# A Mamba scan on four engines: which of its products run on GpSimd, who makes the joins, and where z's SiLU stands

## The chip, the core and the metric

The kernel runs on one core of a Trainium2 chip. It is written instruction by instruction: each engine (TensorE, VectorE, ScalarE, GpSimd) and SyncE's DMA queue carries out its own instructions in the order in which the program issues them, and semaphores hold an instruction back until what it reads is there and what it overwrites is no longer needed. The metric is the time of one execution on the device in microseconds; for several runs the median is given. In the profile TensorE is PE (its weight loads PEld), VectorE is DVE, ScalarE is ACT, GpSimd is POOL and SyncE is SP.

## What is computed

A two-layer model on a 64 x 64 image of 256 channels, all in float32. Layer 0 is convolutions followed by an attention over 4096 positions. Layer 1 treats the positions as 4096 tokens: a Mamba block that runs forward and backward over them, with a small MLP behind it, and then a mixture of two experts. The change touches the Mamba block alone. Cut to what matters, the reference there is

```python
xz = einsum(x, in_proj_w); xc, z = split(xz)           # 512 channels each
xc = silu(causal_conv4(xc))
dt, Bm, Cm = split(xc @ x_proj_w); dt = softplus(dt @ dt_proj_w + b)
dA = exp(dt[..., None] * A); dBx = dt[..., None] * Bm * xc[..., None]
h = dA_t * h + dBx_t                                   # 512 channels x 16 states, step by step over the tokens
y = sum_over_states(h * C_t) + xc * D
out = (y * silu(z)) @ out_proj_w
```

once with the tokens in order and once reversed. The two results are added (m), and a layer norm, two matrix products and another layer norm follow.

## The kernel before

**Iterations and slots.** The tokens are cut into 8 chunks of 512, and the two directions take turns, so `mamba_phase` runs over 16 iterations: iteration i works on direction i % 2. The 512 channels by 16 states of an iteration are cut into 32 slots (`slots`, `SPS` = 32): four channel tiles e, in each of them four groups of states k, in each of them two halves j. A slot holds 128 rows (32 channels by 4 states) twice over, as [128, 2, 512]. The slot's number within its iteration is called `at` in the code. All 512 slots run in one loop, and the loop body writes out the order of the work on every engine by hand: the scheduler adds semaphores, and moves nothing.

**What a slot n does.**

- *Input product* (`inflow`, L1931, GpSimd): u = dtx * B into one of three buffers `dbx`. It is issued two slots ahead, in slot n - 2, and a buffer comes free when the scan of slot n - 1 relative to the issue has ended.
- *Decays* (`decay`, L1921, ScalarE): two exponentials of 512 elements into one of two PSUM buffers `da`, issued one slot ahead.
- *Scan* (`recur`, L1942, VectorE): the recurrence over both halves in one instruction of 1024 elements.
- *Join* (`bring`, L1967, VectorE): the scan takes both halves in one run, so the second half of the next slot needs its old state added to its first column, a 128x1 addition into `dbx`. It is issued right behind scan n for slot n + 1, and only from iteration 2 on, when there is an old state. The value to add (`brought`) is prepared by `carry` on GpSimd and ScalarE in slots 9 to 11, 30 and 31.
- *State copy* (`keep`, L1973, ScalarE): the last column of the scan, one slot later, ahead of the decays.
- *Product* with C: in most slots on VectorE (`readout`, L1953), behind the scan and the join. The slots in the set `POOLED` have it on GpSimd (`pooled`, L1958); there the scan writes straight to an SBUF buffer `h` (four of them), and the product is issued one slot later, behind that slot's input product. These are called pooled slots here, and the others plain.
- *Sums over states* (`sum_states`, L1982, TensorE), two slots at a time; if the first of the two is pooled, they are issued one slot later. The *gate product* (`close`, L1991, VectorE) multiplies the finished y of a channel tile by silu(z), in slots 1, 9, 17 and 25.

The loop body carries the order, for example:

```python
inflow(n + 2)
if n > 0:
    keep(n - 1)
if n > 0:
    decay(n + 1)
recur(n)
```

**What runs in between.** `prepare` computes the next iteration's xc, dt and z in small steps, one per slot (five of them early, in the last five slots of the iteration before): input projection, four convolution blocks on TensorE in slots 3 to 6 with a ScalarE pass after each, xc's SiLU in slot 8 (L1392 with a table load before and one behind it, L1331), the pieces of dt in slots 12 to 27 (among them L1438, L1441 and L1447 on ScalarE, the dt product L1499 on GpSimd in slots 21, 23, 25 and 27, and its stores to HBM, L1503). z's SiLU stands in slot 28 (L2055, again with two table loads). `output` is the output projection of the iteration before, in slots 1 to 3 (L1557 on TensorE).

`load_dt` (L1542, SyncE's queue) reads the rows of dt and dt*x back from HBM, each spread over 128 partitions, into one of three buffers for each; such a load waits until the last reader of its buffer is done. The second load for the next iteration takes the buffer that the decay and the input product of slot 30 read last.

`tail` is what follows the Mamba block on a finished chunk: two layer norms and the MLP, spread over about two iterations. It moves on by one step per slot, and each step names the engine it needs; `FULL` lists for every engine the slots in which no such step may be taken.

## Time and profile before

| | |
|---|---|
| median of 3 runs | 4116.03 us |
| the runs | 4113.85, 4116.03, 4123.45 us |
| the profiled execution | 4112.53 us |
| its span (first to last instruction) | 4110.7 us |
| mean granted TensorE clock | 0.933 |
| first scan to last scan of the Mamba stage | 1934.0 to 3812.6 us |

One execution is profiled. In a row of instruction groups stand the line, engine, operation, what is written and read with shapes, the count, then the busy microseconds and the mean nanoseconds of one instruction, and last the engine's idle time just before them and what ended it. A row of the stage table has the stretch, its length, then busy time and count for PE, PEld, DVE, ACT and POOL, the granted clock, and the DMA engines' busy share and GB/s. A row of waits has who waited for whom: microseconds in total, times, longest. A row of the timeline has start and length in microseconds, engine, line, operation, and in brackets the idle time before it with its releaser. An instruction's start may lie up to 0.1 us before the end of the one ahead of it on the same engine.

### The profile page before, as it was taken

To read this page: it belongs to the slowest core of one execution; us is meant where nothing else is said; L and a number is where in the kernel's file an instruction comes from. 1 tells how busy PE (TensorE), PEld (TensorE's weight loads), DVE (VectorE), ACT (ScalarE), POOL (GpSimd) and SP (SyncE) were. 2 spreads that over 40 slices of the span, in tenths; PEclk is the share of its full clock that TensorE was granted. 3 is DMA by queue.
4 is the path that set the end of the run, shared out by engine and by line. 5 is a ranking of instruction groups with operands and counts; after the bars stand their busy time and mean duration, and the time that the engine had idled before them with its cause. 6 is when DMAs were issued, how large, how long until landed. Compare 5 with 4: busy or idle time off the path is not lost. (4 is left out here: it accounts for less than half of the span.)

```text
span 4110.7 us, 44059 instructions
## 1 busy us (share of the span) xinstructions
PE 3590.8 (87%) x14968; PEld 1196.7 (29%) x14968; DVE 3501.4 (85%) x3335; ACT 2568.4 (62%) x3841; POOL 1807.0 (44%) x1137
## 2 busy tenths in 40 slices
PE   6769888999999999997888888888888888886898
PEld 2324332222222222222222222222222222222444
DVE  8998777989888889877899999999999999999322
ACT  1111226988888878875777767677777767774222
POOL 3020000000000000002888888888988888888100
PEclk9889998999999999998889999999999999987999
DMA  6232215222322223214333344444334444442121
GB/s 208 93 101 94 81 58 157 51 64 61 66 62 59 61 63 63 53 40 145 126 105 108 108 137 121 131 126 124 115 111 109 140 119 128 126 127 80 57 62 55
DMA packets 164329, 399.98 MB, mean 97 GB/s; under 512 B 36997, under 2 KB 46469, under 8 KB 163838
## 3 DMA queue, kind: packets, MB, share of 16 engines
q1 hardware_dynamic: 137166, 304.26, 24.5%
q0 software_dynamic: 24624, 84.43, 8.9%
q10 hardware_dynamic: 2304, 8.39, 0.6%
q8 instruction: 119, 1.95, 0.2%
q14 instruction: 116, 0.95, 0.1%
HBM read 268.17 MB, written 79.56 MB: 85 GB/s over the span
## 5 line engine op out<-in xcount | busy, mean ns | idle before, releaser
L1931 POOL TENSOR_TENSOR dbx<-dtxr,b 128x1024 f32<-128x1024 f32 x512 | 1202.0, 2360 | 232.8 <-DVE dbx L1967 92.1
L1044 ACT ACTIVATE e<-sc 128x1024 f32<-128x1024 f32 x1024 | 994.2, 1023 | 166.4 <-PE sc L1037 141.7
L1942 DVE TENSOR_TENSOR_SCAN da<-da,state,dbx 128x1024 f32<-128x1024 f32 x400 | 940.3, 2351 | 52.6 <-ACT da L1921 43.9
L954 DVE TENSOR_TENSOR s<-s,e 128x1024 f32<-128x1024 f32 x768 | 880.2, 1218 | 19.2 <-ACT e L1044 18.7
L1921 ACT ACTIVATE da<-dtr,aneg 128x512 f32<-128x512 f32 x1024 | 708.3, 692 | 50.4 <-DVE h L1942 18.7
L1037 PE MATMUL sc<-q,kS 32*128 32x512 f32 x4096 | 647.9, 645 | 16.2 <-ACT e L1044 11.4
L961 PE MATMUL av<-e,vT 128*32 128x512 f32 x4096 | 552.5, 608 | 0.2
L977 POOL DMA_DIRECT2D s<-s x94 | 81.5, 874 | 943.0 <-DVE s L954 872.8
L1953 DVE TENSOR_TENSOR h<-da,c 128x1024 f32<-128x1024 f32 x400 | 488.7, 1222 | 5.0 <-DVE dbx L1967 0.6
L462 PE MATMUL cv<-v,u 128*128 128x512 f32 x928 | 412.8, 605 | 29.4 <-DVE pad L283 14.2
L1982 PE MATMUL y<-h,sel 128*32 128x512 f32 x2048 | 312.5, 627 | 40.1 <-POOL h L1958 20.3
L1037 PEld LDWEIGHTS sc<-q,kS 32*128 32x128 f32 x4096 | 211.0, 184 | 455.1 <-issue 249.4
L1342 PE MATMUL mm<-u,win 128*128 128x512 f32 x464 | 253.1, 685 | 84.7 <-ACT xp L1370 77.7
L1973 ACT COPY state<-da 128x2 f32<-128x2 f32 x399 | 64.5, 162 | 359.0 <-DVE h L1953 358.0
L1958 POOL TENSOR_TENSOR h<-h,c 128x1024 f32<-128x1024 f32 x112 | 263.5, 2353 | 46.9 <-ACT state L1973 46.9
L1942 DVE TENSOR_TENSOR_SCAN h<-da,state,dbx 128x1024 f32<-128x1024 f32 x112 | 262.5, 2343 | 25.2 <-ACT da L1921 13.6
L462 PEld LDWEIGHTS cv<-v,u 128*128 128x128 f32 x928 | 178.7, 194 | 261.3 <-issue 227.8
L560 DVE SCALAR_TENSOR_TENSOR acc<-pad,wdw_s,acc 128x768 f32<-128x768 f32 (+1 forms) x192 | 236.0, 1234 | 19.9 <-ACT acc L553 14.2
L1388 PE MATMUL mm<-xp,taps 128*128 128x512 f32 x480 | 212.7, 595 | 0.0
L143 POOL TENSOR_TENSOR ln_few<-ln_few,minus_half 128x4 f32<-128x4 f32 x29 | 34.5, 1190 | 397.7 <-DMA ln_few<-ln_row 259.4
L954 DVE TENSOR_TENSOR s<-e 128x1024 f32<-128x1024 f32 x128 | 152.0, 1219 | 58.6 <-ACT e L1044 58.5
L961 PEld LDWEIGHTS av<-e,vT 128*32 128x32 f32 x4096 | 81.8, 108 | 395.2 <-issue 385.9
(380 smaller groups left out, 3902.6 us busy)
## 6 DMA issues: line engine op xcount, KB each, us to landing
dtr<-dtd SPq DMA_DIRECT2D x128, 512.0 KB
dtxr<-dtd SPq DMA_DIRECT2D x128, 512.0 KB
s<-s POOLq DMA_DIRECT2D x94, 512.0 KB, 5.8
b<-bcd SPq DMA_DIRECT2D x64, 256.0 KB
c<-bcd SPq DMA_DIRECT2D x64, 256.0 KB
dtd<-dt SPq DMA_DIRECT2D x64, 256.0 KB
dtd<-few SPq DMA_DIRECT2D x64, 256.0 KB
u<-uv SPq DMA_DIRECT2D x24, 640.0 KB
```

The lines of the kernel that those rows point to most:

```text
L462: nc.tensor.matmul(rows4(ps), u[:, dy, P * ci : P * ci + P], v[:, dy : dy + HR, ci, :], start=dy + ci == 0, stop=dy == k - 1 and ci == CT - 1,
L954: nc.vector.tensor_tensor(z, x, y, ALU.add)
L961: nc.tensor.matmul(g.av[32 * h : 32 * h + 32, :], vT[:, kb, P * t + 32 * h : P * t + 32 * h + 32], es[h // 2][:, h % 2, :], start=kb == 0, ...
L1037: nc.tensor.matmul(ps[h // 2][:, h % 2, :], kS[r, t, P * kb : P * kb + P], q_t[r, t, :], start=True, stop=True,)
L1044: nc.scalar.activation(e, ps[i], AF.Exp)
L1342: nc.tensor.matmul(ps, win[d][:, t, P * e : P * e + P], u[:, t, ::-1] if d else u[:, t, :], start=t == 0, stop=t == CT - 1,)
L1921: nc.scalar.activation(da[:, v, :], dts[i, e, j][0][:, v, :], AF.Exp, scale=aneg[i % 2][:, a : a + 1])
L1931: nc.gpsimd.tensor_tensor(u, dts[i, e, j][1], bcs[i, k][0][:, None, :].to_broadcast([P, 2, N]), ALU.mult)
L1942: nc.vector.tensor_tensor_scan(das[n].rearrange("p v n -> p (v n)"), da.rearrange("p v n -> p (v n)"), u.rearrange("p v n -> p (v n)"), st ...
L1953: nc.vector.tensor_tensor(hs[n], das[n], bcs[i, k][1][:, None, :].to_broadcast([P, 2, N]), ALU.mult)
L1958: nc.gpsimd.tensor_tensor(hs[n], hs[n], bcs[i, k][1][:, None, :].to_broadcast([P, 2, N]), ALU.mult)
L1982: nc.tensor.matmul(ys[i, e][32 * j : 32 * j + 32, :], cx.sel, hs[n + j // 2][:, j % 2, :], start=False, stop=k == SQ - 1,)
```

## The change

Four things are edited. `POOLED` goes from seven slots to eight: 8 and 28 leave it, 0, 6 and 30 join it. In a pooled slot n the join for slot n + 1 is no longer issued on VectorE behind the scan; it is issued on ScalarE as an Identity activation with the old state as its bias, between the state copy and the decays. z's SiLU moves from slot 28 to slot 24 (not in iteration 0, where it stays). The slot lists that keep the tail's steps off ScalarE and GpSimd are rewritten: for ScalarE 24 and 25 stand in the place of 28, for GpSimd 1 and 7 in the place of 9 and 29.

By these lists the tail's steps fall, from its second run on, into other slots. In even iterations its VectorE reduction (L1620) goes from slot 4 to slot 10, its GpSimd multiplies (L149) from slots 3 and 22 to 6 and 29, its two ScalarE passes on the norm (L1587) from 23 to 30. In odd iterations the VectorE subtraction (L129) goes from slot 24 to 29, and the last two MLP additions (L1613) from 16 and 23 to 25 and 28.

```diff
@@ recur @@
-            bring(n + 1)
+            if n % SPS not in POOLED:
+                bring(n + 1)
@@ bring @@
-            x = us[n][:, 1, 0:1]
-            nc.vector.tensor_scalar(x, x, brought[i, e // 2][:, e % 2, j // 2, k : k + 1], None, ALU.add)
+            x, old = us[n][:, 1, 0:1], brought[i, e // 2][:, e % 2, j // 2, k : k + 1]
+            if (n - 1) % SPS in POOLED:
+                nc.scalar.activation(x, x, AF.Identity, bias=old)
+            else:
+                nc.vector.tensor_scalar(x, x, old, None, ALU.add)
@@ mamba_phase @@
-        POOLED = {4, 8, 10, 12, 16, 20, 28}
+        POOLED = {0, 4, 6, 10, 12, 16, 20, 30}
...
-            "ACT": {6, 7, 8, 9, 16, 17, 18, 19, 22, 28, 29, 31},
-            "POOL": {5, 9, 11, 13, 17, 21, 23, 25, 27, 29, 30, 31},
+            "ACT": {6, 7, 8, 9, 16, 17, 18, 19, 22, 24, 25, 29, 31},
+            "POOL": {1, 5, 7, 11, 13, 17, 21, 23, 25, 27, 30, 31},
@@ the loop over the slots @@
                 if n > 0:
                     keep(n - 1)
+                if at in POOLED:
+                    bring(n + 1)
                 if n > 0:
                     decay(n + 1)
                 recur(n)
...
-                if at == 28 and i + 1 < 2 * NCH:
+                if at == (24 if i > 0 else 28) and i + 1 < 2 * NCH:
                     for z in gots[i + 1]["z"]:
                         nc.scalar.activation(z, z, AF.Silu)
                     exp_and_log()
```

## The prediction

> **What bounds the kernel now.** First the page: busy shares, then the costliest groups.

> ```profile
> PE 3590.8 (87%) x14968; PEld 1196.7 (29%) x14968; DVE 3501.4 (85%) x3335; ACT 2568.4 (62%) x3841; POOL 1807.0 (44%) x1137
> ...
> L1931 POOL TENSOR_TENSOR dbx<-dtxr,b 128x1024 f32<-128x1024 f32 x512 | 1202.0, 2360 | 232.8 <-DVE dbx L1967 92.1
> L1942 DVE TENSOR_TENSOR_SCAN da<-da,state,dbx 128x1024 f32<-128x1024 f32 x400 | 940.3, 2351 | 52.6 <-ACT da L1921 43.9
> L1953 DVE TENSOR_TENSOR h<-da,c 128x1024 f32<-128x1024 f32 x400 | 488.7, 1222 | 5.0 <-DVE dbx L1967 0.6
> L1958 POOL TENSOR_TENSOR h<-h,c 128x1024 f32<-128x1024 f32 x112 | 263.5, 2353 | 46.9 <-ACT state L1973 46.9
> ```

> The Mamba stage runs from 1931 to 3815 us: 512 slots, each with one scan on VectorE (2.35 us) and one product (1.22 us on VectorE, 2.35 on GpSimd). The table of stages, taken from 2400 to 3600 us, and the waits of VectorE there show what limits it.

> ```profile
> 2400.00:3600.00 1200.00, 1016.66 (x2974) 340.76 (x2973) 1146.66 (x1004) 861.36 (x1580) 1022.33 (x539) 0.93 0.42 122
> ```
> ```profile
> DVE da L1942 <- ACT da L1921: 21.2, 15, 1.7
> DVE h L1942 <- ACT da L1921: 10.7, 10, 1.2
> ```

> VectorE is 96% busy, GpSimd 85%, ScalarE 72%. What VectorE waits for is mostly ScalarE's decays. So VectorE is the bound, with holes. I therefore read the timeline scan by scan. The first view is VectorE in slots 28 to 30 of iteration 6, the second ScalarE there, the third two scans of iteration 1, which has no joins.

> ```profile
> 2976.47 2.34 DVE L1942 TENSOR_TENSOR_SCAN h<-da,state,dbx 128x1024 f32<-128x1024 f32 x1
> 2978.73 0.19 DVE L1967 TENSOR_SCALAR dbx<-dbx,brought 128x1 f32<-128x1 f32 x1
> ...
> 2979.49 2.35 DVE L1942 TENSOR_TENSOR_SCAN da<-da,state,dbx 128x1024 f32<-128x1024 f32 x1
> ...
> 2984.38 2.36 DVE L1942 TENSOR_TENSOR_SCAN da<-da,state,dbx 128x1024 f32<-128x1024 f32 x1 [1.20 <-ACT da L1921]
> ```
> ```profile
> 2976.79 1.42 ACT L1921 ACTIVATE da<-dtr,aneg 128x512 f32<-128x512 f32 x2
> 2978.22 1.28 ACT L2055 ACT_TABLE_LOAD   x1
> 2979.52 2.00 ACT L2055 ACTIVATE z<-z 128x1024 f32<-128x1024 f32 x2
> 2981.54 1.28 ACT L1331 ACT_TABLE_LOAD   x1
> ...
> 2982.93 1.41 ACT L1921 ACTIVATE da<-dtr,aneg 128x512 f32<-128x512 f32 x2
> ```
> ```profile
> 2088.08 2.35 DVE L1942 TENSOR_TENSOR_SCAN h<-da,state,dbx 128x1024 f32<-128x1024 f32 x1 [1.99 <-PE y L1982]
> 2090.35 2.33 DVE L1942 TENSOR_TENSOR_SCAN da<-da,state,dbx 128x1024 f32<-128x1024 f32 x1
> ```

> From one scan's start to the next I read, over iterations 2 to 14 and without idle time: 3.52 to 3.60 us in a plain slot, 2.55 in a pooled one. In iteration 1 the same are 3.52 to 3.60 and 2.26. So a join costs nothing in a plain slot (the product behind it is ready to follow) and 0.29 in a pooled one, where the next scan stands behind it. An iteration takes 117.6 us, 4.4 of it idle: 1.41 in slot 29 (behind z's SiLU), 1.05 in slot 9 (behind xc's SiLU), 0.64 in slot 4, 0.57 in slot 19 (TensorE's sums), 0.41 in slot 0.

> **The change part by part**, per iteration, for iterations 2 to 15. The sum is made on the profiled execution: 4112.5 us, span 4110.7; the median shown is 3.5 above it.

> *One product more on GpSimd.* Pooled slots go from 7 to 8; each saves 3.58 - 2.55 = 1.03 on VectorE: **-1.0**. GpSimd gains 2.35 beside it. It is 85% busy, so 2.35 in some 115 us makes 88%; that cover fails only where GpSimd is already late, which is slot 0, below.

> *Eight joins on ScalarE.* 8 x 0.29 = **-2.3** on VectorE, if the next scan is not held up. ScalarE in a pooled slot: the state copy starts 0.12 after the scan, the two decays end 1.73 after it. A join goes between them. The trace has no such form; the nearest rows are the 128x1 copy at L1447 (0.16) and the 128x16 exponential at L1521 (0.20) on one side, the 128x512 Identity with bias at L1384 (0.69) on the other. I take 0.20, the nearest in size: decays end at 1.95, the next scan can start at 2.26. At 0.69 they end at 2.42 and each pooled slot loses 0.16, 18 us in all. Behind the join in ScalarE's queue stand decay n+1 and all that follows, and the join waits for GpSimd's input product n+1. That one ends, relative to the scan's start, at -3.3 in slot 4, -2.2 in 6, -3.0 in 10, -0.2 in 12 (at worst 0.9), -0.5 in 16, -2.2 in 20, -2.4 in 30 (medians), so it has been done by then. In slot 0 it ends at +2.0.

> [...]

> *z's SiLU from slot 28 to slot 24.* It is four instructions, 4.66 us on ScalarE (two table loads of 1.28, two SiLUs), and no DMA. Its old hole goes: **-1.4**. In slot 24 it stands ahead of a dt copy with its one-column copy (0.58 + 0.16), state copy 24, and decay 26 (1.42). With decay 25 ending 1.73 after scan 24, decay 26 ends at 1.73 + 4.66 + 0.74 + 0.17 + 1.42 = 8.75, where VectorE, with scan 24, 25 and the gate product of slot 25 (0.68), gets to scan 26 after 3.59 + 4.10 = 7.7, or 8.4 with a tail step in odd iterations. So a new hole of 0.35 to 1.05; and decays that run late, as in even iterations now (up to 3.6 after scan 24), make it 2.65. I take **+1.1**, as the tail step that causes the worst is moved away. GpSimd's dt product of slot 25 and the dtd stores of SP then wait some 3 us for that dt copy; the row-broadcast loads they precede are needed from slot 30 on, so this costs nothing; if it did, it would show in slot 0.

> *Slots 1 to 9.* Here plain VectorE time is not the bound: TensorE goes without a gap from the gate product of slot 1 through output projection and four convolution blocks of 3.5 us (8 matmuls each), then xc's SiLU (4.5 us on ScalarE), then decay 10. From the end of that product to scan 10 is 30.3 to 32.2 us in every iteration. The change saves VectorE 0.29 in slot 4, 1.3 in slot 6 and gives back 1.0 in slot 8; a 1.2 us reduction of the tail leaves slot 4 every second iteration and comes back in slot 10. That is 1.2 of savings a turn, of which the chain lets through only the wait of ScalarE's slot-8 state copy, 0.28 to 1.21, mean 0.6. The rest turns into idle time: **+0.6** (0 to 1.2).

> *The turn of the iteration.* Slot 0's second input row waits for a buffer that decay 30 frees, then for its DMA. The views are SP's issues and GpSimd in iteration 6.

> ```profile
> 2984.37 0.51 SPq L1542 DMA_DIRECT2D dtr<-dtd  x1
> 2984.97 0.56 SPq L1542 DMA_DIRECT2D dtxr<-dtd  x1
> ```
> ```profile
> 2990.84 7.00 POOL L1931 TENSOR_TENSOR dbx<-dtxr,b 128x1024 f32<-128x1024 f32 x3 [2.32 <-DMA dtxr<-dtd]
> ```

> From issue to use are 5.0 to 7.7 us (here 5.9). With the SiLU gone decay 30 ends 1.73 after scan 29 and no longer 4.85, but slots 29 and 30 also shrink, by 1.5 and 1.3. Input product 1 then ends 1.73 + 0.6 + 6.4 + 2.36 = 11.1 after scan 29, scan 32 is at 3.6 + 2.3 + 3.6 = 9.5 (10.7 with a tail step of 1.2): 0.4 to 1.6 into slot 0. Join, two decays and hand-overs add 1.75, now in series, where VectorE waited for the product alone before. Slot 0 takes 2.3 to 3.4 and at worst 4.7, mean 3.05, so idle 0.8 for 0.41: **+0.4** (-0.4 to +2). Then product 30 on GpSimd pushes input product 2 to 4.7 after input product 1; VectorE's join in slot 1 waits up to 0.75: **+0.5**. The sums of slot 30 now stand in slot 1 of TensorE's queue, ahead of that gate product; they are ready about 1 us before VectorE is.

> *Tail slots.* The tail's instructions are the same, moved by some slots; the 2.35 us GpSimd multiply falls into slots 6 and 29 for 3 and 22. Input products there are 1 to 3 us early, so nothing; without that lead 2.35 a turn at most.

> Sum: -1.0 - 2.3 - 1.4 + 1.1 + 0.6 + 0.4 + 0.5 = -2.1 an iteration, 14 iterations: -29.4. Iterations 0 and 1 have no joins and stalls of their own; I take 0. From 4116.0 that is **4086.6**. All good ends together give -4.75 an iteration (4050), all bad ones +1.9 (4143).

> [...]

> **The rivals.** *The joins block ScalarE (slower).* If the wait for GpSimd is later than I read, for instance on a later instruction of its queue, the decay and the next scan slip one for one. It speaks for it that GpSimd ends 0.8 to 1.2 after the scan in slots 11 and 13, between the pooled ones; against it the medians above. My slack is 0.3; beyond it, 0.3 of lateness in each of seven slots eats the 2.1. With 0.9 beyond the slack the iteration is 6.3 - 2.1 = 4.2 longer: 4175; with 0.45, 4130. Chance 0.13.

> *The turn takes it.* Late DMA and GpSimd's backlog, with slot 0 at 4.7 and slot 1 at its full 0.75 each time: +1.9 more, 4113. For it: the row's wait is in the trace already; against: decay 30 comes earlier. Chance 0.12.

> *TensorE hides it.* If the TensorE and ScalarE chain of slots 1 to 9 is fed from further back than slot 1, the gain before it is absorbed and only slots 10 to 24 keep theirs (4 x 0.29): -1.2 + 1.1, about 4115. Against: VectorE has no idle time in slots 21 to 28. Chance 0.11.

> *All good ends*, 4050 to 4060: chance 0.05. My forecast, 4062 to 4108: 0.59.

> **How the numbers follow.** A time within 0.2% (8.2 us) can hardly be told from no change. Faster: 0.59 + 0.05 + half of the second and some of the third, 0.72; same 0.12; slower 0.16. The range goes from 4060 to 4120.

> **What would show it.** Pooled slots of 2.26 with a ScalarE Identity 128x1 ahead of the decays; no hole in slot 29; a hole at scan 26 behind the SiLU; slots 1 to 9 nearly as long as before; idle time of VectorE near 5.6 an iteration. Long gaps ahead of the joins on ScalarE would make me wrong.

## The result: 26 us slower, where 29 us less was forecast

The changed kernel takes 4142.2 us (median of 5 runs, 4141.0 to 4153.7), the kernel before 4116.0. The ratio is 1.0076, with a 95% interval of 1.0059 to 1.0093. All runs below are given by such a ratio to the kernel before, and a difference in us between two of them is the difference of their ratios times 4116. The forecast was 4086.6 and its range ended at 4120. The profiled executions have spans of 4139.1 and 4110.7 us, 28.4 apart. Single executions of one kernel lie up to some 20 us apart (4104.8 to 4127.1 in one run below), so places are read from the one profiled execution, and gains from the ratios.

The page of the kernel after, first its busy shares, then the groups that answer to those shown of before (columns: line, engine, operation, tiles, shape, count, busy us, mean ns of one, then the idle time ahead of them and what ended most of it):

```profile
PE 3597.1 (87%) x14968; PEld 1194.4 (29%) x14968; DVE 3466.7 (84%) x3207; ACT 2571.2 (62%) x3953; POOL 1845.6 (45%) x1153
...
L1931 POOL TENSOR_TENSOR dbx<-dtxr,b 128x1024 f32<-128x1024 f32 x512 | 1203.4, 2362 | 172.7 <-DMA dtxr<-dtd 65.6
...
L1942 DVE TENSOR_TENSOR_SCAN da<-da,state,dbx 128x1024 f32<-128x1024 f32 x384 | 901.1, 2347 | 86.4 <-ACT da L1921 81.1
...
L1954 DVE TENSOR_TENSOR h<-da,c 128x1024 f32<-128x1024 f32 x384 | 469.0, 1221 | 4.6 <-DVE da L1942 0.5
L1986 PE MATMUL y<-h,sel 128*32 128x512 f32 x2048 | 316.2, 653 | 128.8 <-POOL h L1959 110.5
```

The same group of sums in the kernel before:

```profile
L1982 PE MATMUL y<-h,sel 128*32 128x512 f32 x2048 | 312.5, 627 | 40.1 <-POOL h L1958 20.3
```

VectorE has 34.7 us less to do (3501.4 before) and the scans of the plain slots wait more: 86.4 us where it was 52.6. New is the last line. TensorE's sums over states waited 20 us for GpSimd's products before, and 110 after.

From 2400 to 3600 us, the row of the stage table (PE, PEld, DVE, ACT and POOL busy, then clock, DMA share and GB/s) and the waits (total us, times, longest):

```profile
2400.00:3600.00 1200.00, 1005.81 (x2937) 335.51 (x2936) 1110.89 (x901) 858.17 (x1653) 1033.57 (x544) 0.92 0.40 121
```
```profile
PE y L1986 <- POOL h L1959: 76.7, 25, 7.9
ACT xc L1384 <- PE mm L1388: 66.4, 38, 3.2
DVE da L1942 <- ACT da L1921: 52.4, 30, 4.2
```

VectorE's idle time in this stretch is 89 us (1200 - 1110.9), before it was 53. The three waits can be read as one chain, which the runs below take apart: the sums wait for GpSimd, ScalarE's passes over the convolution (L1384) wait for TensorE (66.4; 27.6 before), and VectorE's scans wait for the decays behind those passes (52.4; 21.2 before).

The table sets the forecast's terms beside the trace. It gives the mean of iterations 3 to 14, per iteration, from scan start to scan start; idle time is VectorE's, and hand-overs of about 0.1 us beside a join (0.29 less the join's own 0.19) count as work.

| step of the prediction | forecast | measured |
|---|---|---|
| VectorE's own work (one product, eight joins) | -3.3 | -2.9 |
| hole in slot 29 goes | -1.4 | -1.4 |
| new hole behind z's SiLU (slots 23 to 25) | +1.1 | +0.5 |
| slots 1 to 9, idle | +1.1 | +2.5 (slot 6 alone +2.0) |
| slot 0, idle | +0.4 | +1.2 |
| slots 10 to 22, idle | 0 | +0.5 (slot 20 +0.8, slot 19 -0.5) |
| slot 31, idle | 0 | +0.7 |
| sum, from the unrounded terms | -2.1 | +1.0 |

That is 11.8 us over twelve iterations. Iteration 2 is 5.4 longer, iteration 15 4.9, iterations 0 and 1 together 2.9, and 3.5 lie outside; together 28.4. VectorE's idle time is 8.4 us an iteration, where the prediction had some 5.6.

VectorE behind z's SiLU, and from slot 28 on, in the iteration that the prediction shows (counted from 0 it is iteration 8; the prediction called it 6):

```profile
2984.26 2.36 DVE L1942 TENSOR_TENSOR_SCAN da<-da,state,dbx 128x1024 f32<-128x1024 f32 x1 [0.78 <-ACT da L1921]
...
2994.92 2.35 DVE L1942 TENSOR_TENSOR_SCAN da<-da,state,dbx 128x1024 f32<-128x1024 f32 x1
...
2998.51 2.34 DVE L1942 TENSOR_TENSOR_SCAN h<-da,state,dbx 128x1024 f32<-128x1024 f32 x1
3000.77 2.33 DVE L1942 TENSOR_TENSOR_SCAN da<-da,state,dbx 128x1024 f32<-128x1024 f32 x1
```

The hole is at scan 26 (0.78), scan 29 starts without one, and pooled slot 30 takes 2.26. So far the change does what was forecast. ScalarE's join behind scan 30:

```profile
2998.63 0.16 ACT L1977 COPY state<-da 128x2 f32<-128x2 f32 x1 [0.89 <-DVE h L1954]
2998.69 0.30 ACT L1969 ACTIVATE dbx<-dbx,brought 128x1 f32<-128x1 f32 x1
2998.88 1.41 ACT L1921 ACTIVATE da<-dtr,aneg 128x512 f32<-128x512 f32 x2
```

It takes 0.30 where the prediction took 0.20 from a row. The decays still end before the scan does (at 3000.29, the scan at 3000.85), as the sum had it.

### The profile page after: what moved, and what is told of

It is laid out like the page before. It is cut to its first block, busy times and chain, and to the rows that moved or that the text cites. A ratio compares the mean times of both kernels' runs of the same rounds, so it can differ in the third digit from the quotient of the medians.

```text
span 4139.1 us, 44001 instructions
## 1 busy us (share of the span) xinstructions
PE 3597.1 (87%) x14968; PEld 1194.4 (29%) x14968; DVE 3466.7 (84%) x3207; ACT 2571.2 (62%) x3953; POOL 1845.6 (45%) x1153
## 3 DMA queue, kind: packets, MB, share of 16 engines
q8 instruction: 119, 1.95, 0.2%
## 4 chain that ended last, share of the span: by engine, by line
PE 37%; DVE 14%; ACT 10%; issue 9%; DMA 3%; POOL 3%; SPq 0%; DVEq 0%; POOLq 0%; ACTq 0%
PE sc L1037 8%; DVE da L1942 8%; PE av L961 7%; PE mm L1388 5%; ACT da L1921 4%; PE mm L1557 3%; PE mm L2250 3%; PE o L2192 2%; DVE h L1954 2%; DVE h L1942 2%; PE y L1986 2%; DVE s L954 1%; PE mm L1435 1%; DMA dtxr<-dtd 1%; POOL dbx L1931 1%
## 5 line engine op out<-in xcount | busy, mean ns | idle before, releaser
L1931 POOL TENSOR_TENSOR dbx<-dtxr,b 128x1024 f32<-128x1024 f32 x512 | 1203.4, 2362 | 172.7 <-DMA dtxr<-dtd 65.6
L1942 DVE TENSOR_TENSOR_SCAN da<-da,state,dbx 128x1024 f32<-128x1024 f32 x384 | 901.1, 2347 | 86.4 <-ACT da L1921 81.1
L1921 ACT ACTIVATE da<-dtr,aneg 128x512 f32<-128x512 f32 x1024 | 706.9, 690 | 43.0 <-DVE h L1942 15.7
L1954 DVE TENSOR_TENSOR h<-da,c 128x1024 f32<-128x1024 f32 x384 | 469.0, 1221 | 4.6 <-DVE da L1942 0.5
L1942 DVE TENSOR_TENSOR_SCAN h<-da,state,dbx 128x1024 f32<-128x1024 f32 x128 | 299.8, 2342 | 33.1 <-ACT da L1921 21.6
L1959 POOL TENSOR_TENSOR h<-h,c 128x1024 f32<-128x1024 f32 x128 | 301.5, 2355 | 8.4 <-ACT state L1977 8.4
L1342 PE MATMUL mm<-u,win 128*128 128x512 f32 x464 | 237.3, 647 | 28.4 <-ACT xp L1370 20.8
```

Source lines behind the costliest of these rows:

```text
L1921: nc.scalar.activation(da[:, v, :], dts[i, e, j][0][:, v, :], AF.Exp, scale=aneg[i % 2][:, a : a + 1])
L1931: nc.gpsimd.tensor_tensor(u, dts[i, e, j][1], bcs[i, k][0][:, None, :].to_broadcast([P, 2, N]), ALU.mult)
L1942: nc.vector.tensor_tensor_scan(das[n].rearrange("p v n -> p (v n)"), da.rearrange("p v n -> p (v n)"), u.rearrange("p v n -> p (v n)"), st ...
L1954: nc.vector.tensor_tensor(hs[n], das[n], bcs[i, k][1][:, None, :].to_broadcast([P, 2, N]), ALU.mult)
L1959: nc.gpsimd.tensor_tensor(hs[n], hs[n], bcs[i, k][1][:, None, :].to_broadcast([P, 2, N]), ALU.mult)
```

## The turn: what stands in front of TensorE

The turn into iteration 8: TensorE in the changed kernel, GpSimd just before it, then TensorE in the kernel before:

```profile
2892.99 1.56 PE L1986 MATMUL y<-h,sel 128*32 128x512 f32 x8 [4.44 <-POOL h L1959]
2894.49 8.28 PE L1557 MATMUL mm<-xc,wout 128*128 128x512 f32 x16
...
2904.56 3.70 PE L1388 MATMUL mm<-xp,taps 128*128 128x512 f32 x8
```
```profile
2888.29 2.35 POOL L1931 TENSOR_TENSOR dbx<-dtxr,b 128x1024 f32<-128x1024 f32 x1 [2.41 <-DVE da L1942]
2890.60 2.34 POOL L1959 TENSOR_TENSOR h<-h,c 128x1024 f32<-128x1024 f32 x1
```
```profile
2875.30 2.84 PE L1557 MATMUL mm<-xc,wout 128*128 128x512 f32 x6
2881.24 1.12 PE L1557 MATMUL mm<-xc,wout 128*128 128x512 f32 x2 [3.10 <-DVE xc L1991]
...
2887.69 3.60 PE L1388 MATMUL mm<-xp,taps 128*128 128x512 f32 x8
```

Before, six passes of the output projection ran ahead of the gate product. After, the sums of slot 30 stand in front of all of it, and they wait for GpSimd's product 30, which stands in GpSimd's queue behind an input product that waits itself: 2.41 us here, for a buffer that a scan frees; 3.62 at the next turn, for its DMA. Only then does the projection start. The granted clock shows in the rows too: eight sums take 1.06 us elsewhere, 1.56 here and 1.9 at most turns. In iterations 3 to 14 a period of half clock (0.5 in the trace's record of the granted clock) begins in slots 0 to 2 in 11 of 12 iterations (61 us in all), before in 3 (10 us). The convolution starts 8.6 us after the end of the gate product; before, 7.2 in even and 6.5 in odd iterations (means of iterations 2 to 14).

Four runs alter this place. The first takes slot 28 instead of 30:

```diff
-        POOLED = {0, 4, 6, 10, 12, 16, 20, 30}
+        POOLED = {0, 4, 6, 10, 12, 16, 20, 28}
```

> The changed kernel with the pooled slots 0, 4, 6, 10, 12, 16, 20 and 28: 28 for 30, the number stays eight. Theory A: the sums of slot 30 are back in slot 0, TensorE is not held up, 1.6 to 2 us an iteration less: 4114 to 4120. Theory B: slot 0's join stays in series with the late input product; a plain slot 30 gives the DMA 1.3 us more, of which half shows: 4133. Theory C: no difference, 4142.

Measured: 1.0006 (0.9991 to 1.0022). One slot's number is worth 0.7%, some 29 us. In the profiled execution even iterations fall to 113.2 us (after 116.5, before 118.1), and there the convolution starts 6.4 after the gate product. Odd ones stay at 121.1 (after 120.9, before 117.3) and the convolution at 8.5: their slot 0 is still late, and the last sections return to it. The swap also takes a product from GpSimd at the turn. VectorE's wait for an input product in slot 1, 0.5 us an iteration in the changed kernel as forecast, goes with it, so the 29 us are not TensorE's order alone.

To see whether slot 0's serial join is the loss, slot 28 takes the place of slot 0, and then of both 0 and 30 (seven products):

```diff
-        POOLED = {0, 4, 6, 10, 12, 16, 20, 30}
+        POOLED = {4, 6, 10, 12, 16, 20, 28, 30}     # the one
+        POOLED = {4, 6, 10, 12, 16, 20, 28}         # the other
```

> The changed kernel with the pooled slots 4, 6, 10, 12, 16, 20, 28 and 30: 28 for 0. Theory A: the sums of slot 30 are still in slot 1 behind GpSimd, so the loss of slots 1 to 9 stays: 4135 to 4142. Theory B: slot 0's join is back on VectorE, decay 1 runs beside the input product; idle time of slot 0 goes from 1.6 to 0.4, 14 x 1.2 = 17 us less: 4125. Theory C: no difference.

> The changed kernel with seven pooled slots, 4, 6, 10, 12, 16, 20 and 28: neither 0 nor 30. One product an iteration goes back to VectorE (+1.0). Theories A and B together: both holes at the turn go, 1.6 + 1.2 - 1.0 = 1.8 us an iteration less, 4117 or below; the six joins on ScalarE that stay are worth 0.3 each against before, so it may fall below 4116. Theory C: 4142 or more.

Measured: 1.0071 (1.0051 to 1.0091) and 1.0033 (1.0019 to 1.0047). Without slot 0 in the set nothing is won while slot 30 is in it. Slot 0 itself loses 1.0 us of idle time (1.65 to 0.68), but slot 31 gains 0.7 and slot 4 0.8, the latter through a decay buffer (below), so this run alone doesn't clear slot 0. Without slot 30, slot 0's product on GpSimd is a gain: 1.0006 with it, 1.0033 without, with intervals that just overlap. So slot 30 in the set is a loss, and slot 0 without it is none.

Two runs keep slot 30 and mend TensorE's order. One puts three matmuls of the output projection ahead of the sums of slot 30, as they ran before:

```diff
                 for f in range(ET):
+                    if co == 0 and f == ET - 1:
+                        yield
...
+                if at == 1 and i > 0:
+                    out = output(i - 1)
+                    step(out)
                 if j == 2 and n > 2 and (n - 3) % SPS in POOLED:
                     sum_states(n - 3)
```

> The changed kernel with one thing moved: the first three of the four matmul pairs of the output projection's first half are issued ahead of the sums of slot 30 in TensorE's queue, not behind them. Nothing else differs. Theory A (the sums of slot 30, now in slot 1 and waiting for GpSimd's product 30, hold TensorE's queue up and start output projection and convolutions some 2 us later, so that scan 10 is late): the stretch from slot 1's gate product to scan 10 goes from 32.1 back to about 30.5 us, 14 x 1.6 = 22 us less, 4120. Theory B (the join of slot 0 on ScalarE, in series behind GpSimd's late input product, is the loss): no difference, 4142. Theory C (the SiLU in slot 24 and the moved tail steps): no difference, 4142.

Measured: 1.0051 (1.0039 to 1.0064), about 10 us back. Theory A had 22. The convolution still starts 8.2 to 8.3 after the gate product, and the half clock still begins there in 10 of 12 iterations. The other adds five matmuls ahead of the sums, whose result the true ones overwrite:

```diff
+                if co == 0:
+                    for v, f in enumerate((0, 1, 2, 0, 1)):
+                        nc.tensor.matmul(
+                            ps, wout[d][:, f, P * co : P * co + P], g[:, f, :], start=v == 0, stop=v == 4
+                        )
+                    yield
```

> The changed kernel in which TensorE is kept busy through the wait of slot 1: five extra matmul pairs of the output projection (into the same PSUM tile, overwritten by the true ones, so the result is the same) ahead of the sums of slot 30, and the first two true pairs between those sums and the gate product. Theory A2 (the wait for product 30 leaves TensorE idle, its granted clock halves for 3.4 to 10 us at the turn of every iteration, and the output projection and the first convolution run at half rate): no half clock in slots 0 to 2 any more; gate product to first convolution from 8.5 to about 6.5 us, and 14 x 1.6 to 2 us less than the changed kernel, which is 31 us above before: 4 to 9 us above before. Theory A1 (only the order in the queue counts, the clock does not): as the run that moved three pairs forward, 20 us above before, or more for the extra 4.7 us of matmuls.

Measured: 1.0033 (1.0015 to 1.0051), 18 us back and 14 above before, between the two theories. The half clock in slots 0 to 2 falls from 61 to 7 us and the convolution starts at 7.2 to 7.6. Between this run and the one above the intervals overlap, so how much of it is the clock and how much the order is not settled.

## Parts of the change alone

Only the joins on ScalarE, with the seven products, z's SiLU and the lists of before:

```diff
-            bring(n + 1)
+            if n % SPS not in POOLED:
+                bring(n + 1)
...
+            if (n - 1) % SPS in POOLED:
+                nc.scalar.activation(x, x, AF.Identity, bias=old)
...
+                if at in POOLED:
+                    bring(n + 1)
```

> The kernel before with the joins behind its seven pooled slots on ScalarE and nothing else of the change. My price of 0.29 a join where nothing else holds the next scan, in slots 10, 12, 16 and 20 (slots 4, 8 and 28 are followed by waits on TensorE's chain or on a SiLU): 4 x 0.29 x 14 = 16 us below before. Rival (the joins block ScalarE's queue): no gain, or above before.

Only the new tail lists:

```diff
-            "ACT": {6, 7, 8, 9, 16, 17, 18, 19, 22, 28, 29, 31},
-            "POOL": {5, 9, 11, 13, 17, 21, 23, 25, 27, 29, 30, 31},
+            "ACT": {6, 7, 8, 9, 16, 17, 18, 19, 22, 24, 25, 29, 31},
+            "POOL": {1, 5, 7, 11, 13, 17, 21, 23, 25, 27, 30, 31},
```

> The kernel before with the two new slot lists of the tail steps and nothing else of the change. Theory D (the moved tail steps put a DMA round trip and a GpSimd multiply into SP's and GpSimd's queues just before the turn, so the loads for slots 31 and 0 leave some 3 us late, and an MLP pass into pooled slot 20): idle time in slot 20 (odd) 1.5, in slot 31 (even) 1, in slot 0 (odd) 1 more: +1.8 us an iteration on average, 20 to 25 us above before. Rival (the steps are the same and lie where there is room): within 4 us of before.

And the kernel with 28 for 30, but with the old lists (the same lines the other way round):

> The changed kernel with 28 for 30 in the pooled set, and with the two slot lists of before. Against the same with the new lists (4 us above before or level with it): theory D: the odd iterations lose the idle time of slots 20, 29 and 0, the even ones that of slot 31, together 2 us an iteration, but the two norm passes are back in slot 23 right ahead of the SiLU, which costs 0.8: 14 x 1.2 = 17 us less, 13 to 17 us below before. Rival (the lists make no difference): level with before.

Measured: joins alone 1.0026 (1.0016 to 1.0036), lists alone 0.9991 (0.9979 to 1.0002), old lists with the SiLU in slot 24 1.0044 (1.0031 to 1.0058). The lists cost nothing by themselves, and the SiLU in slot 24 needs them: with the old ones tail steps stand beside it, slot 25 of even iterations takes 6.8 us and slot 0 7.5. So theory D was wrong in both runs.

The joins alone are a loss, where 16 us less had been expected, though pooled slots shrink as forecast (slots 8 and 10 from 2.55 to 2.27). Slot 20 of odd iterations gives the hint. It takes 3.88 us in this kernel and in the changed one, and 2.55 before. ScalarE in slot 20 of iteration 7 of the changed kernel:

```profile
2843.69 0.16 ACT L1977 COPY state<-da 128x2 f32<-128x2 f32 x1 [0.18 <-DVE h L1954]
2843.75 0.30 ACT L1969 ACTIVATE dbx<-dbx,brought 128x1 f32<-128x1 f32 x1
2845.95 1.42 ACT L1921 ACTIVATE da<-dtr,aneg 128x512 f32<-128x512 f32 x2 [1.90 <-DVE h L1942]
```

The decays of slot 21 wait 1.90 us for the end of scan 20, which they have no business with: there are two decay buffers, and slot 21 should use the one that slot 19 left. In the built program it doesn't. There the tile for slot 21 has the PSUM address of the tile of slot 20.

## The decay buffers do not take turns

The text on the kernel before says that the scheduler adds semaphores and moves nothing. It does one thing more, which I had not looked at: it picks one of the two `da` buffers for each tile. Where it gives a slot the buffer of the slot just before, decays and scans run one after the other. The built programs show where, in iterations 2 to 15: before, slot 5 of odd iterations (7 times); joins alone and lists alone, slot 5 (6 times each) and slot 21 (6 and 5) of odd iterations; the changed kernel, slot 7 of all iterations (13) and slot 21 of odd ones (6). All of these follow a pooled slot. Of the kernels of the section on the turn, 28 for 30, the one with neither and the two with TensorE's order mended repeat buffers in iterations 2 to 15 just as the changed kernel does, so their comparison does not rest on this. The one with 28 for 0 repeats in slot 5 of odd iterations as well.

The trace of before shows its own repeat, on ScalarE in slot 4 of iteration 7, with the same wait in all seven odd iterations from 3 on:

```profile
2774.04 1.42 ACT L1921 ACTIVATE da<-dtr,aneg 128x512 f32<-128x512 f32 x2 [2.10 <-DVE h L1942]
```

That is the 0.64 of slot 4, which the prediction lists without a cause.

Two names with one buffer each force turns. The order of the instructions on every engine stays the same. (Two tiles behind the steady part of the loop get one of the names each; not shown.)

```diff
-            da = das[n] = pda.tile([P, 2, N], FP, name="da", tag="da")
+            da = das[n] = pda.tile([P, 2, N], FP, name="da", tag=f"da{n % 2}", bufs=1)
```

This went into four kernels: the changed one, the one before, 28 for 30, and the joins alone.

> The changed kernel, with the decay tiles named by turns (two names with one buffer each, chosen by the parity of the slot), in place of one name with two buffers of which the program picks one. The order of the instructions stays as it is on every engine; only buffers and waits differ. In the built program of the changed kernel the decays of slot 21 in odd iterations, and of slot 7 in all, lie in the buffer of the decays just before them, so they can only start when the scan before them has ended; in the kernel before only slot 5 of odd iterations has this. Theory F (the broken turn costs time): slot 20 of odd iterations goes from 3.88 to about 2.3, 1.5 us in six iterations, so 9 us less: about 4133. Slot 6 gains little, because its decay also waits behind a convolution pass. Theory G (VectorE is held up elsewhere anyway, by z's SiLU in slot 25 or by the turn): the same time as the changed kernel, 4142, with the hole found again in slot 23 to 25.

> The kernel before, with decay tiles by turns. Only slot 5 of odd iterations changes: its decays no longer wait for scan 4 (1.4 us in seven iterations). Theory F: at most 9.7 us less, 4106. Theory H (slots 1 to 9 are bound by the chain of TensorE's output projection and convolution and xc's SiLU, so that what VectorE gains there is lost again in slot 9): the same as before, within 3 us, with slot 9 longer by 1.3 in odd iterations. I expect H.

> The changed kernel with slot 28 in GpSimd's set in place of slot 30, which took as long as before by itself (ratio 1.0006), now with decay tiles by turns. Theory F: slot 20 of odd iterations gives back 1.5 in six iterations, and slot 6 of even iterations up to 0.3 in seven: 9 to 11 us less, about 4104, faster than the kernel before by some 0.2%. Theory G: no change from 1.0006.

> The kernel before with its seven joins moved to ScalarE and nothing else, which took 1.0026 of the time before where the sum said 0.996, now with decay tiles by turns. Theory F: the 1.33 of slot 20 in odd iterations comes back, 8 us, so a ratio near 1.0007; that the joins still give no gain would then be the chain of slots 1 to 9 and the holes behind both SiLUs, which take what is saved ahead of them. Theory I (a ScalarE join is itself what delays the decays of slot 21, not the buffer): slot 20 of odd iterations stays at 3.88 and the ratio at 1.0026.

| kernel | as it was | by turns |
|---|---|---|
| changed | 1.0076 (1.0059 to 1.0093) | 1.0040 (1.0026 to 1.0055) |
| before | 1 | 0.9987 (0.9977 to 0.9997) |
| 28 for 30 | 1.0006 (0.9991 to 1.0022) | 0.9944 (0.9924 to 0.9963) |
| joins alone | 1.0026 (1.0016 to 1.0036) | 0.9966 (0.9953 to 0.9978) |

The same slot 20 of iteration 7 in the changed kernel by turns:

```profile
2860.34 0.30 ACT L1969 ACTIVATE dbx<-dbx,brought 128x1 f32<-128x1 f32 x1
2860.54 1.41 ACT L1921 ACTIVATE da<-dtr,aneg 128x512 f32<-128x512 f32 x2
```

The decays follow the join at once and slot 20 takes 2.26 us. The buffers cost 15 us in the changed kernel, 26 in the one with slot 28, 25 with the joins alone and 5 before. Theory F holds and theory I falls. The sizes are above what F gave (8 to 11 us): in the profiles slot 20 alone gives back 10 us (six odd iterations by 1.6), and where all of the rest comes from is not shown. Slot 6, the largest row of the table, turns out to have two causes, each of which is enough: the repeated buffer, and a convolution pass that waits for TensorE ahead of the decays, as here in slot 6 of iteration 8 of the changed kernel by turns:

```profile
2928.85 0.69 ACT L1384 ACTIVATE xc<-mm,small 128x512 f32<-128x512 f32 x1 [2.54 <-PE mm L1388]
...
2929.67 1.42 ACT L1921 ACTIVATE da<-dtr,aneg 128x512 f32<-128x512 f32 x2
```

In even iterations 28 for 30 alone leaves it at 3.9 us and turns alone at 4.2; with both it takes 2.5. Slot 9 then takes 1.1 of that back. In odd iterations it stays at 4.5 even so. In the kernel before, slot 4 of odd iterations falls from 3.83 to 2.55 and slot 7 takes it back (3.60 to 4.87), as theory H has it, though in slot 7 and not 9.

By turns the joins can be priced: 0.9966 with them on ScalarE, 0.9987 without, 9 us for the 28 that 7 x 0.29 x 14 makes (the intervals just overlap). VectorE's work falls by 1.7 us an iteration there, and its idle time grows by 1.1, in slots 0, 3, 7, 9 and 29.

The version with 28 for 30 and turns beats both kernels: 0.56% faster than before. It differs from the changed kernel by those two edits, and they are worth 54 us.

## What was still open: z's SiLU, the clock, SyncE's queue

z's SiLU in slot 24 and the new lists, in the kernel before by turns:

```diff
-                if at == 28 and i + 1 < 2 * NCH:
+                if at == (24 if i > 0 else 28) and i + 1 < 2 * NCH:
```

> The kernel before with decay tiles by turns (ratio 0.9987), and in addition only z's SiLU in slot 24 and the new tail lists; joins and GpSimd's seven products stay as they were. Theory J (the step as the prediction has it): -1.4 for the hole in slot 29, +1.1 or less for the one at scan 26, so 4 to 8 us less than by turns alone, a ratio of 0.997 to 0.998; slot 29 falls to 3.6 in a plain slot and slot 25 is near 5. Theory K (the SiLU in slot 24 costs more than its old place, because the tail's reductions now stand at the turn and slot 0 grows): 5 to 15 us more than by turns alone, 1.000 to 1.002, with slot 0 of odd iterations near 5.

Measured: 1.0001 (0.9988 to 1.0014), 6 us more than by turns alone, with intervals that overlap. The time is K's, at its low end; the holes are J's. The old hole goes (slot 29 of even iterations 4.88 to 3.60) and the new one is small (0.4 of idle time in slot 25). But slot 0 of odd iterations grows from 3.6 to 4.7 and iteration 15, which drains the tail, from 112.1 to 119.8. The lists alone, without turns, have these at 4.3 and 116.1, so the moved tail steps have a part in it; the SiLU's own part is not shown.

Next, the clock in the kernel with 28 for 30 by turns, whose TensorE stands still for 4.62 us in odd iterations and then runs ten passes in 7.23:

```profile
2762.90 2.84 PE L1557 MATMUL mm<-xc,wout 128*128 128x512 f32 x6
2770.36 7.23 PE L1557 MATMUL mm<-xc,wout 128*128 128x512 f32 x10 [4.62 <-DVE xc L1995]
```

Six extra matmuls fill that time, in another run two (the same lines as in the run with five, with the other counts):

> The kernel with products {0, 4, 6, 10, 12, 16, 20, 28} and decay tiles by turns (ratio 0.9944), with six more matmuls of the output projection in slot 1, whose sums are overwritten by the true ones, and two true ones behind them: they leave out nothing and only keep TensorE at work while it waits for the gate product. In odd iterations TensorE now idles 4.6 us there, and the ten matmuls after it take 0.72 us each where six before it took 0.47. Theory L (TensorE's granted clock halves after that idle time, and the convolution starts later by it): the convolution starts 1.4 us earlier in odd iterations, counted from the gate product, the low clock in slots 0 to 2 goes from 31 us to under 10, and the time falls by 6 to 10 us, ratio near 0.992. Theory M (the halved clock there is hidden, and the wait of slot 6 has another cause): the same 0.9944 or a little more, as the extra matmuls also cost time.

> As the run with six extra matmuls, which were too many: each is two passes of 0.45 us, so they took 5.4 us and pushed the three true ones that ran ahead of the gate product behind it. Now two extra ones (1.9 us) and then three true ones ahead of the gate product, as without them. Nothing is left out. In odd iterations TensorE's idle time ahead of the gate product falls from 4.6 to about 2.7 us, and nothing true is pushed back. Theory L (the halved clock after the idle time costs time): the ten passes after the gate product take 0.45 us each and not 0.72, so the convolution starts 1.4 to 2.5 us earlier in odd iterations than with decay tiles by turns alone (8.03 after the gate product), slot 6 of odd iterations shrinks by as much, and the time falls by 6 to 15 us: ratio 0.991 to 0.993. Theory M (hidden): the convolution earlier, but the same 0.9944, the gain found again in slot 9 or in the turn. Theory N (an idle time of 2.7 us is still enough for the clock to fall): 8.0 and 0.9944 as without.

Measured: 1.0046 (1.0029 to 1.0064) and 0.9947 (0.9930 to 0.9963). Six were a mistake of mine. Each matmul is two passes (the six stand as 12 in the trace), so they took 5.4 us and pushed true work back; the run says that the half clock can be kept away (31 to 3 us), and nothing on its price. With two the half clock falls from 31 to 17 us and the convolution of odd iterations starts at 7.6 for 8.0, and the time is the same. Here is iteration 7 with two:

```profile
2762.61 2.74 PE L1565 MATMUL mm<-xc,wout 128*128 128x512 f32 x6
2767.47 6.25 PE L1565 MATMUL mm<-xc,wout 128*128 128x512 f32 x10 [2.13 <-DVE xc L2003]
```

Even 2.13 us without work are followed by slow passes, 0.63 each for 0.46. So theory N has a part in it, and the price of the clock alone stays below what these runs resolve.

Last, the turn from even to odd iterations. SyncE's queue in the changed kernel:

```profile
2987.78 0.38 SPq L145 DMA_DIRECT2D ln_inv<-ln_few  x1
2993.57 0.32 SPq L146 DMA_DIRECT2D ln_rstd<-ln_inv  x1
2993.94 0.53 SPq L1542 DMA_DIRECT2D dtr<-dtd  x1
...
2996.31 0.53 SPq L1509 DMA_DIRECT2D first_r<-first_row  x1
```

L145 and L146 belong to a layer norm of the tail, which now runs in slot 26. L146 reads what L145 stores, so it stands 5.8 us at the head of the queue with the next iteration's loads behind it. GpSimd and VectorE then wait for them:

```profile
3001.96 0.22 POOL L1519 TENSOR_TENSOR brought<-aneg,first_r 128x16 f32<-128x16 f32 x1 [2.62 <-DMA first_r<-first_row]
...
3008.29 2.34 POOL L1931 TENSOR_TENSOR dbx<-dtxr,b 128x1024 f32<-128x1024 f32 x1 [3.62 <-DMA dtxr<-dtd]
```
```profile
3004.70 0.21 DVE L1971 TENSOR_SCALAR dbx<-dbx,brought 128x1 f32<-128x1 f32 x1 [1.60 <-POOL brought L1524]
```

One run issues L146 a tail step later, in the kernel with 28 for 30 by turns:

```diff
-    nc.sync.dma_start(out=rstd, in_=inv.to_broadcast([P, N]))
+    if not rest:
+        nc.sync.dma_start(out=rstd, in_=inv.to_broadcast([P, N]))
     for at in range(1 + rest):
         yield "POOL" if at == rest else "DMA"
+        if rest and at == 0:
+            nc.sync.dma_start(out=rstd, in_=inv.to_broadcast([P, N]))
```

> The kernel with products {0, 4, 6, 10, 12, 16, 20, 28} and decay tiles by turns (ratio 0.9944); in the tail's layer norms the second DMA of the way there and back (L146, ln_rstd<-ln_inv) is issued one tail step later than the first (L145), not right behind it. In the changed kernel L146 stands in SyncE's queue from slot 26 of even iterations on and waits 5.8 us for L145 to land, and the next iteration's loads of dt, dt*x and the first columns stand behind it. Theory O (that wait is what makes the joins of slot 31 and the input products of the next slot 0 late): slot 31 of even iterations goes from 4.7 to about 3.6, slot 0 of odd ones from 5.2 to about 4.2, 2.1 us in six or seven turns, 8 to 14 us in all: ratio 0.991 to 0.9925. Theory P (the second load for slot 0 waits for the buffer that decay 30 frees, whatever stands ahead of it): slot 31 may shrink, slot 0 stays near 5.2, and the ratio at 0.994.

Measured: 0.9946 (0.9930 to 0.9963). Slot 0 of odd iterations falls from 5.23 to 3.28, more than theory O said, and slot 6 behind it from 4.45 to 3.55; but slot 31 of even iterations grows from 4.71 to 5.64, where O had it shrink. The place is shown; a gain in the whole time is not, as these two ratios resolve some 10 us.

## Why the prediction was wrong, step by step

- *VectorE's own work*: right as work. Pooled slots take 2.26, and 2.9 of the 3.3 came. The decays end before the scan does, though the join is 0.30 long and not 0.20.
- *z's SiLU*: the holes went where it said, the new one smaller (+0.5 for +1.1). (The terms given for decay 26 add up to 8.72, not 8.75.) With the lists, and without the rest of the change, it still gave no gain: slot 0 of odd iterations and iteration 15 took it.
- *"The sums of slot 30 ... are ready about 1 us before VectorE is"*: this step failed most. The sentence itself held: in iterations 2 to 14 the sums end 0.5 to 1.4 us ahead of the gate product. But it looked only at whether VectorE would wait, and not at what stands behind those sums in TensorE's own order: the output projection, the convolution, xc's SiLU and the decays. The sums wait up to 7.9 us for GpSimd there, and six passes that ran ahead of the gate product now run behind it. Moving the product to slot 28 gives 29 us, and 40 with buffers by turns (1.0040 against 0.9944), some of it through GpSimd's own queue; mending TensorE's order with slot 30 kept gives 10 and 18. The prediction had itself called slots 1 to 9 a chain of TensorE's, and then did not carry the wait into it: +1.1 of idle time forecast, +2.5 measured, of which slot 6 has the buffer as a second cause. Nor was TensorE's granted clock weighed. In this trace the sums wait 3.5 to 7.9 us in 14 of iterations 1 to 15, and half clock in slots 0 to 2 went from 10 to 61 us in twelve iterations; what the clock alone costs no run resolves.
- *Eight joins, "if the next scan is not held up"*: the condition failed, through the buffer that the program picks: 15 us in the changed kernel. The trace of before has the same wait in another slot (2.10 us in slot 4), and it was not followed. By turns the term was still too large in time: the next scan starts earlier, but a later wait takes two thirds of it (9 us for 28).
- *"If it did, it would show in slot 0", and "tail slots ... nothing"*: slot 0 is 1.2 longer for 0.4, slot 31 0.7 for none. The tail's instructions are the same, but one DMA of theirs now stands ahead of the loads. Counting the moved DMA with its wait in SyncE's queue would have pointed there: with that DMA issued later, slot 0 of odd iterations fell by 2.0 us.
- *Iterations 0, 1 and 15 as the rest or at nothing*: iterations 0 and 1 are 2.9 us longer and iteration 15 4.9. The new lists alone make iteration 15 116.1 for 113.3.
- *The rivals*: "the turn takes it" named the right place and sized it too small (4113). "Joins block ScalarE" had the right time, 4130 to 4175, and the wrong mechanism: a join waits long only in slot 0 (28.5 us in 14 joins, 0.9 in all other slots). The sum of all bad ends, 4143, met the measured time by luck, for the terms came out otherwise. Slot 0's product, taken to GpSimd in the kernel with slot 28, was no loss but gained 11 us (1.0033 to 1.0006, intervals that just overlap).

With slot 28 and buffers by turns the kernel is 23 us faster (15 to 31), near the 29 forecast. That nearness does not confirm the sum: turns alone give 5 of the 23, the joins 9 of 28, and the SiLU with the lists none. What the runs show is that the placing of one product and the choice of the decay buffers, together 54 us, turned a gain into a loss.

## What to carry to other kernels

When work moves to a slower engine (here a product takes 2.35 us on GpSimd and 1.22 on VectorE), follow who reads its result in that reader's own order: here the instructions queued behind the reader paid for the wait (TensorE's sums waited 110 us for GpSimd, 20 before), not the engine that was relieved. When tiles with different lives share a ring of buffers, look in the built program which buffer each one gets, and force turns where a pipeline depends on them (15 us in the changed kernel). A moved step takes its DMAs along, and here one that stood 5.8 us at the head of SyncE's queue held up the loads behind it.
